# Attention in bursts of seven energy tiles: fewer periods, one movable accumulator bank

## The chip, the cores and the metric

The kernel runs on one core of one Trainium2 chip. Its engines are TensorE (matmuls; its weight loads are counted apart as PEld), VectorE (DVE), ScalarE (ACT), GpSimd (POOL) and SyncE (SP), which here only issues transfers. The metric is the device time of one execution in microseconds (us), from the first to the last instruction. Matrix products land in PSUM, an accumulation memory of eight banks; one bank holds 128 x 512 float32 values. The profile is one execution recorded by the hardware.

## The reference

The input x has 4 images of 64 channels and 96 x 96 pixels, N = 9216 pixels. Two layers follow each other, each preceded by a group normalization. The first is attention over all pairs of pixels, with a sigmoid in place of a softmax, and a channel gate after it:

```python
q = einsum('bchw,oc->bohw', x, wq) + bq   # 8 channels; k likewise, v has 64
energy = einsum('bcn,bcm->bnm', Q, K)     # N x N for each image
att = sigmoid(energy)
out = einsum('bcm,bnm->bcn', V, att) + x
scale = sigmoid(mlp(mean(out)) + mlp(max(out)))
x = x + out * scale
```

The second multiplies 32 x 16 low modes of the image's Fourier transform by complex 64 x 64 weights and transforms back; its result is again added to x. All is float32. The attention is by far the larger part: 4 x 9216 x 9216 sigmoids.

## The kernel before

**Tiling.** Two images make a pair, so there are two pairs (`NPAIR`), with 64 channels of each image on the 128 partitions. A pair's queries are cut into 18 blocks of 512 (`NBLK`, `NB`), which gives 36 blocks in all; its keys into 72 chunks of 128. A block therefore needs 2 x 72 = 144 energy tiles of 128 keys x 512 queries, alternately for one image and the other.

**A period.** The 144 tiles are taken six at a time (`BURST`), 24 bursts to a block and 864 in all. `energies` (L418) issues six matmuls (L424). Each contracts only 32 rows: tile t uses rows 32 * (t % 4) onward, four copies of queries and keys being kept on the four 32-row strips. The six results go to two tiles of three PSUM banks, and two sigmoids on ScalarE (L428), of three banks each, carry them to a buffer `at` in ordinary memory, of which there are two. `attend` (L431) multiplies the values with six sigmoid tiles and adds into an accumulator bank (L435); the tiles of the two images go to its lower and upper 64 partitions. The main loop (L557) issues in period t the energies of burst t + 1, and then the attends of burst t. So the sigmoids of burst t + 1 run beside the attends of burst t.

**The end of a block.** After its last burst VectorE adds the accumulator to x (L578) and takes the maximum (L580).

**Other work.** PSUM has eight banks: six hold energies; the two of the pool `ps_a`, given out by `bank_a` (L357), hold the accumulator and whatever else TensorE has to do. That is written by hand into the lists `mid` (ahead of a period's attends) and `end` (behind them), by period number: keys and values of the chunks (L380, L391), the queries of the next block (L400, three periods ahead of it), normalization and statistics, and, in the second half, the first pair's channel gate and its whole second layer: results (L246), transposes (L258), transform along the width (L267) and the height (L286), mixing with the spectral weights (L186), and the way back (L312, L330). `place` (L508) gives offsets and spacings. The weights of the mixing are loaded into four buffers of 512 KB, four loads a group, ten periods apart (L533); a group's mixing stands six and nine periods behind its load (L535).

The framework places semaphores between engines. It may also reorder instructions that its own model takes to be not ready. What follows the main loop, the second pair's second layer, is a tail of its own.

Of the kernel before, what the change touches and what calls it, by code (L numbers as in the profile page):

```python
# [33 lines left out]
F32 = mybir.dt.float32  # L34
F32R = mybir.dt.float32r
AF = mybir.ActivationFunctionType
ALU = mybir.AluOpType
AX = mybir.AxisListType
PSUM = bass.MemoryType.PSUM

P = 128
B, C, H, W = 4, 64, 96, 96
N = H * W
NPAIR = B // 2
# [3 lines left out]
KH = 32  # L48
NB = 512
NBLK = N // NB  # L50
NCH = N // P
BURST = 6
PART = 3
BURSTS = 2 * NCH // BURST
SIDE = 4
U = KH * KW * 4
UPAD = 4 * SIDE
STRIP = 8 * W
SQ = 32
NSQ = H // SQ  # L60
NSTRIP = N // STRIP
# [16 lines left out]
def tile_kernel(ctx: ExitStack, tc: tile.TileContext, x, cst, late, spec, out):  # L78
    nc = tc.nc
# [10 lines left out]
    xs = []  # L90
# [9 lines left out]
    vT = xpool.tile([P, NCH, P], F32, tag="vT", name="vT")  # L100
# [131 lines left out]
    class Hidden(Layer1):  # L232
# [25 lines left out]
        def transposes(self, r):  # L258

            pt = self.bank(f"pt_{self.p}_{r}")  # L260
            for i in range(4):
                nc.tensor.transpose(pt[:W, bass.ts(i, P)], xs[self.p][:, bass.ts(4 * r + i, W)],  # L262
                                    ident)
            self.xts[r] = self.work.tile([W, NB], F32, tag="xT", bufs=5, name=f"xT_{self.p}_{r}")
            self.move(self.xts[r], pt[:W, :])

        def along_w(self, m):  # L267
# [78 lines left out]
    with tc.tile_pool(name="work", bufs=1) as work, \  # L346
            tc.tile_pool(name="kv", bufs=1) as kvp, \
            tc.tile_pool(name="q", bufs=2) as qp, \
            tc.tile_pool(name="att", bufs=2) as attp, \
            tc.tile_pool(name="ps_s", bufs=1, space=PSUM) as ps_s, \  # L350
            tc.tile_pool(name="ps_a", bufs=2, space=PSUM) as ps_a:

        eb = [ps_s.tile([P, PART, NB], F32, tag=f"e{i}", name=f"e{i}") for i in range(2)]

        kT = kvp.tile([P, NCH // 2, P], F32R, tag="kT", name="kT")

        def bank_a(name):  # L357
            return ps_a.tile([P, NB], F32, tag="a", name=name)

        def halves(src, bias, name):  # L360

# [7 lines left out]
        mark = [None]  # L369
# [6 lines left out]
        def later(step):  # L376
            with tc.issue_after(mark[0].ins):
                step()
# [12 lines left out]
        def values_of(p, s):  # L391
            pp = bank_a(f"pv_{p}_{s}")
            for i in range(4):
                nc.tensor.matmul(pp[:, bass.ts(i, P)], xs[p][:, bass.ts(4 * s + i, P)],  # L394
                                 named("wv"), start=True, stop=True)
            nc.vector.tensor_tensor(  # L396
                vT[:, 4 * s:4 * s + 4, :], pp.rearrange("p (i m) -> p i m", m=P),
                named("bv").unsqueeze(1).to_broadcast([P, 4, P]), ALU.add)
# [16 lines left out]
                    nc.vector.tensor_copy(q[to:to + 32, cols], q[of:of + 32, cols])  # L415
            return q

        def energies(p, n, g, q):  # L418


            for i in range(BURST):
                t = BURST * g + i
                r = 32 * (t % 4)
                nc.tensor.matmul(eb[i // PART][:, i % PART, :], kT[r:r + 32, t // 4, :],  # L424
                                 q[r:r + 32, :], start=True, stop=True)
            at = attp.tile([P, BURST, NB], F32, tag="att", name=f"at_{p}_{n}_{g}")
            for h in range(BURST // PART):
                nc.scalar.activation(at[:, bass.ts(h, PART), :], eb[h], AF.Sigmoid)  # L428
            return at

        def attend(acc, g, at):  # L431
            for i in range(BURST):
                j, b = (BURST * g + i) // 2, i % 2
                half = slice(b * C, (b + 1) * C)
                nc.tensor.matmul(acc[half, :], vT[:, j, half], at[:, i, :],  # L435
                                 start=(j == 0), stop=(j == NCH - 1))

        def stats_of(p):
# [47 lines left out]
        keys(0, 1)  # L486
        values_of(0, 1)

        T = NPAIR * NBLK * BURSTS
        mid = [[] for _ in range(T)]  # L490
        end = [[] for _ in range(T)]
        for s in range(2, NBLK):
            end[s - 2] += [lambda s=s: keys(0, s)]
            mid[s - 1] += [lambda s=s: values_of(0, s)]
            if s + 1 < NBLK:
                end[s - 2] += [lambda s=s: later(norm0[s + 1])]
        each, norm1, mv1 = stats_of(1)
        for i, step in enumerate(each + norm1):
            end[(2 + i // 3) * BURSTS + 2] += [lambda step=step: later(step)]
        last = (NBLK - 1) * BURSTS  # L500
        for s in range(NBLK):
            t = last + -(-(4 * s + 1) // 3)
            end[t] += [lambda s=s: keys(1, s)]
            mid[t + 1] += [lambda s=s: values_of(1, s)]

        first = NBLK * BURSTS

        def place(offset, every, steps):  # L508
            for i, step in enumerate(steps):
                end[first + offset + every * i] += [lambda step=step: later(step)]  # L510

        gate, steps, _ = after(0)
        place(2, 2, steps)
        l1 = Hidden(0, gate, bank_a, lambda dst, src: nc.vector.tensor_copy(dst, src), work)  # L514
        x1d = dram.tile([P, N], F32, tag="x1", name="x1d")
        place(9, 3, [lambda s=s: (l1.result(s), nc.sync.dma_start(
            x1d[:, bass.ts(s, STRIP)], xs[0][:, bass.ts(s, STRIP)])) for s in range(NSTRIP)])
        place(13, 2, [lambda r=r: l1.transposes(r) for r in range(H // 4)])
        place(22, 8, [lambda m=m: l1.along_w(m) for m in range(H // 16)])
        place(64, 2, l1.stats_steps())  # L520

        def workspace():
            ws = xpool.tile([P, N], F32, tag="x0", name="ws")
            l1.ut = ws[:, :U + UPAD]
            at = 2080
            l1.wts = [ws[:, at + 1024 * i:at + 1024 * (i + 1)] for i in range(4)] * (KH // 4)
            l1.vms = [ws[:, at + 4096:at + 5120]] * (KH // 4)
            l1.z = ws[:, at:at + 3072].rearrange("q (h m) -> q h m", m=P)

        place(76, 1, [workspace])  # L530
        place(80, 4, [lambda i=i: l1.along_h(i) for i in range(4)])
        place(98, 1, [l1.constant_mode])
        place(100, 10, [lambda q=q: l1.weights(range(4 * q, 4 * q + 4)) for q in range(KH // 4)])  # L533
        for half in range(2):
            place(106 + 3 * half, 10, [lambda q=q, half=half: l1.mix(q, half)  # L535
                                       for q in range(KH // 4)])
        place(200, 3, [lambda i=i: l1.back_h(i // 4, i // 2 % 2, i % 2) for i in range(8)])
        place(244, 3, [lambda i=i: l1.back_w(i, x1d) for i in range(H // 4)])


        early = []
# [4 lines left out]
            for i, w in enumerate(early):  # L546
                nc.gpsimd.dma_start(w, spec[NSLOT + i])

        place(340, 1, [fetch])
        again = vT.rearrange("p j m -> p (j m)")  # L550
        for s in range(NSTRIP):
            end[T - BURSTS + 2 * s + 1] += [lambda s=s: nc.sync.dma_start(
                again[:, bass.ts(s, STRIP)], xf[bass.ts(1, P), bass.ts(s, STRIP)])]

        at = energies(0, 0, 0, q)
        qn = None
        for t in range(T):  # L557
            p, n, g = t // (NBLK * BURSTS), t // BURSTS % NBLK, t % BURSTS
            nxt = None
            if t + 1 < T:  # L560
                p1, n1, g1 = (t + 1) // (NBLK * BURSTS), (t + 1) // BURSTS % NBLK, (t + 1) % BURSTS
                if g1 == 0:
                    q = qn
                nxt = energies(p1, n1, g1, q)
            for step in mid[t]:
                step()
            if g == 0:
                acc = bank_a(f"acc_{p}_{n}")
            attend(acc, g, at)
            at = nxt  # L570
            if g == BURSTS - 4 and t + 4 < T:
                m = t // BURSTS + 1
                qn = queries(m // NBLK, m % NBLK)
            for step in end[t]:
                step()
            if g == BURSTS - 1:
                blk = xs[p][:, bass.ts(n, NB)]
                nc.vector.scalar_tensor_tensor(blk, acc, 1.0, blk, ALU.mult, ALU.add,  # L578
                                               accum_out=sums[p][:, n:n + 1])
                mark[0] = nc.vector.tensor_reduce(maxs[p][:, n:n + 1], blk, AX.X, ALU.max)  # L580
        gate, steps, f = after(1)
        for step in steps:
            step()
# [2 lines left out]
    with tc.tile_pool(name="tail", bufs=1, reuse_waits="tile") as tail, \  # L586
# [49 lines left out]
        for s in range(NSTRIP):  # L636
# [9 lines left out]
                pa = pa_bank.tile([P, 2 * NB], F32, tag="a", name=f"pa_{n}", bufs=2)  # L646
            v = xt.rearrange("q (h n c) -> q n h c", n=NSQ, c=SQ)
            for k in range(NSQ):
                last = nc.tensor.matmul(pa[:, bass.ts(i, STRIP // NSQ)], fw[:, bass.ts(k, P)], v[:, k],  # L649
                                 start=(k == 0), stop=(k == NSQ - 1))  # L650
            if i < NSTRIP // NSQ - 1:
                continue

# [73 lines left out]
        z = tail.tile([P, P, SQ], F32, tag="z", name="z_1")  # L727
        for i in range(4):
            for b in range(2):
                nc.vector.transpose(z[:H, b * C + i * NO:b * C + (i + 1) * NO, :], pz[b][i][:H, :].rearrange(  # L730
                    "q (k o) -> q o k", o=NO))
        banks.close()
        py_bank = psum("ps_y", 2)
        occupy(2, last, py_bank)
# [100 lines left out]
```

## Time and profile before

The median of three runs is 3196.61 us (3195.66 to 3197.0).

| engine | busy us | share of the span |
|---|---|---|
| TensorE matmuls | 3153.5 | 99% |
| TensorE weight loads, beside matmuls | 1070.9 | 34% |
| ScalarE | 2432.9 | 76% |
| VectorE | 396.4 | 12% |
| GpSimd | 24.5 | 1% |

| group of instructions | number | busy us | mean ns |
|---|---|---|---|
| attends, L435 | 10368 | 2418.1 | 601 |
| sigmoids, L428 | 1728 | 2412.6 | 1448 |
| energies, L424 | 5184 | 636.0 | 461 |
| evacuation of an accumulator, L578 | 36 | 24.9 | 692 |

Each attend is two matmul instructions in the trace (10368 for 5184 tiles). Matmuls overlap, so their mean durations do not add up to time; the distance from one start to the next is what counts. In a timeline line the first number is the start and the second the duration, both in us; the brackets give the idle time of that engine before it, and what ended it.

### The profile page before, as it was taken

The numbers are of one execution on the slowest core, as the hardware profiler recorded it, in microseconds if no ns is written. First come the engines' busy times: TensorE is split into PE (matmuls) and PEld (weight loads), VectorE is DVE, ScalarE is ACT, GpSimd is POOL, SyncE is SP. The second block draws the span as 40 slices with busy tenths as digits, with TensorE's granted clock in tenths as the row PEclk, the third lists the DMA queues.
The fourth block names the chain that finished last, engine by engine and source line by source line (L and its number), as shares of the span: only waits on it lengthen the run. The fifth ranks groups of instructions, "written<-read, shape, count | busy, mean of one in ns | idle before, by whom it ended". The sixth has DMA issues, their size and how long they took to land.

```text
span 3196.5 us, 39125 instructions
## 1 busy us (share of the span) xinstructions
PE 3153.5 (99%) x17490; PEld 1070.9 (34%) x17490; DVE 396.4 (12%) x838; ACT 2432.9 (76%) x1765; POOL 24.5 (1%) x49
## 2 busy tenths in 40 slices
PE   6999999999999999999999999999999999999998
PEld 3333333333333333334333333333333333333336
DVE  4200000000000000002331100000000111000015
ACT  3688888888888888886677777777777777888871
POOL 0000000000000000000000000000000000000001
PEclk9999999999999999999999999999999999999998
DMA  3000000000000000000120100121020102100026
GB/s 139 1 1 1 1 1 1 1 1 1 1 1 1 1 1 1 1 1 1 37 92 17 40 1 30 63 89 37 13 28 10 40 30 70 66 1 1 6 62 221
DMA packets 39145, 88.63 MB, mean 28 GB/s; under 512 B 10336, under 2 KB 17248, under 8 KB 38880
## 3 DMA queue, kind: packets, MB, share of 16 engines
q1 hardware_dynamic: 31856, 61.88, 6.4%
q0 software_dynamic: 5344, 19.27, 1.7%
q10 hardware_dynamic: 1776, 4.97, 0.4%
q8 instruction: 137, 2.24, 0.3%
q14 instruction: 32, 0.26, 0.0%
HBM read 62.77 MB, written 23.33 MB: 27 GB/s over the span
## 4 chain that ended last, share of the span: by engine, by line
PE 98%; DVE 1%; DMA 1%; issue 0%; ACT 0%; POOL 0%; SPq 0%; ACTq 0%
PE acc L435 74%; PE e L424 18%; PE pv L394 1%; PE pv L199 1%; PE py L339 1%; PE pq L405 1%; PE pk L385 1%; DMA x<-in_x_dram 0%; PE py L742 0%; PE pt L262 0%; DVE x L158 0%; DVE xt L641 0%; PE pz L318 0%; PE pu L299 0%; PE pa L272 0%
## 5 line engine op out<-in xcount | busy, mean ns | idle before, releaser
L428 ACT ACTIVATE at<-e 128x1536 f32<-128x1536 f32 x1728 | 2412.6, 1448 | 682.8 <-PE e L424 682.7
L435 PE MATMUL acc<-at,vT 128*64 128x512 f32 x10368 | 2418.1, 601 | 0.0
L435 PEld LDWEIGHTS acc<-at,vT 128*64 128x64 f32 x10368 | 667.8, 136 | 1294.7 <-issue 1279.3
L424 PE MATMUL e<-q,kT 32*128 32x512 f32 x5184 | 636.0, 461 | 1.8 <-ACT at L428 1.3
L424 PEld LDWEIGHTS e<-q,kT 32*128 32x128 f32 x5184 | 257.5, 182 | 642.8 <-issue 595.3
L365 DVE TENSOR_SCALAR full_q<-pq,cs 128x256 f32<-128x256 f32 x36 | 17.4, 484 | 1557.1 <-PE pq L405 1557.0
L578 DVE SCALAR_TENSOR_TENSOR x<-acc,x 128x512 f32<-128x512 f32 x36 | 24.9, 692 | 294.1 <-PE acc L435 294.1
L394 PE MATMUL pv<-cs,x 128*128 128x128 f32 x288 | 42.9, 292 | 0.1
L415 DVE CAST q<-q 32x256 fp32r<-32x256 f32 x144 | 41.0, 285 | 3.8
L341 DVE TENSOR_TENSOR x<-py,x 128x384 f32<-128x384 f32 x24 | 13.4, 558 | 226.0 <-PE py L339 226.0
L394 PEld LDWEIGHTS pv<-cs,x 128*128 128x128 f32 x288 | 35.7, 195 | 14.3 <-DVE full_k L365 12.9
L514 DVE COPY ws<-pv 128x512 f32<-128x512 f32 x16 | 11.1, 691 | 216.4 <-PE pv L199 216.3
L373 DVE SCALAR_TENSOR_TENSOR q<-high_q,cs,full_q 64x256 fp32r<-64x256 f32 x72 | 34.6, 480 | 2.4
L514 DVE COPY xT<-pt 96x512 f32<-96x512 f32 x24 | 16.4, 685 | 114.7 <-PE pt L262 114.7
L365 DVE TENSOR_SCALAR full_k<-pk,cs 128x256 f32<-128x256 f32 x36 | 17.4, 484 | 103.0 <-PE pk L385 103.0
L396 DVE TENSOR_TENSOR vT<-pv,cs 128x512 f32<-128x512 f32 x36 | 24.9, 691 | 8.8 <-PE pv L394 8.8
L580 DVE TENSOR_REDUCE maxs<-x 128x1 f32<-128x512 f32 x36 | 24.7, 685 | 1.1
L385 PE MATMUL pk<-x,cs 128*64 128x256 f32 x144 | 23.3, 395 | 1.5 <-DVE x L145 1.5
L442 DVE BATCH_NORM_STATS2 stats<-x 128x6 f32<-128x512 f32 x36 | 22.3, 679 | 8.1 <-DMA x<-in_x_dram 8.1
L649 PE MATMUL pa<-xt,lc 128*128 128x256 f32 x72 | 19.1, 425 | 3.7 <-DVE xt L641 2.6
L405 PE MATMUL pq<-x,cs 128*64 128x256 f32 x144 | 22.1, 386 | 0.0
L128 PE MATMUL pm_l<-mv_l,cs 128*128 128x1 f32 x8 | 1.7, 286 | 20.6 <-DVE mv_l L124 19.9
(104 smaller groups left out, 457.9 us busy)
## 6 DMA issues: line engine op xcount, KB each, us to landing
ws<-in_spec_dram SPq DMA_DIRECT2D x32, 512.0 KB
x<-in_x_dram SPq DMA_DIRECT2D x15, 512.0 KB
out_dram<-x SPq DMA_DIRECT2D x18, 384.0 KB
w<-in_spec_dram POOLq DMA_DIRECT2D x10, 512.0 KB, 6.6
old<-in_x_dram SPq DMA_DIRECT2D x12, 384.0 KB
x1d<-x SPq DMA_DIRECT2D x12, 384.0 KB
x<-x1d SPq DMA_DIRECT2D x12, 384.0 KB
w_early<-in_spec_dram POOLq DMA_DIRECT2D x9, 512.0 KB, 9.9
```

Of the source, the lines that this page charges most:

```text
L199: self.last = nc.tensor.matmul(pv[bass.ts(g, 32), :].rearrange("q (n k o) -> q n k o", n=SIDE, o=C)[:, :, k, :], self.ut[:, at:at + 32], s ...
L339: nc.tensor.matmul(py[:, :4 * W], self.z[:, i, :], named("gw"), start=True, stop=True)
L365: nc.vector.tensor_scalar(u, src, bias, None, ALU.add)
L373: mark[0] = nc.vector.scalar_tensor_tensor(dst, h.bitcast(F32), is_low, u, ALU.mult, ALU.add)
L385: nc.tensor.matmul(pp[cols, :NB // 2], named("wk")[:, cols], src[:, e, :, :], start=True, stop=True)
L394: nc.tensor.matmul(pp[:, bass.ts(i, P)], xs[p][:, bass.ts(4 * s + i, P)], named("wv"), start=True, stop=True)
L405: nc.tensor.matmul(pq[rows, :half], named("wq")[:, rows], xs[p][:, n * NB + e * half:n * NB + (e + 1) * half], start=True, stop=True)
L415: nc.vector.tensor_copy(q[to:to + 32, cols], q[of:of + 32, cols])
L424: nc.tensor.matmul(eb[i // PART][:, i % PART, :], kT[r:r + 32, t // 4, :], q[r:r + 32, :], start=True, stop=True)
L428: nc.scalar.activation(at[:, bass.ts(h, PART), :], eb[h], AF.Sigmoid)
L435: nc.tensor.matmul(acc[half, :], vT[:, j, half], at[:, i, :], start=(j == 0), stop=(j == NCH - 1))
L514: l1 = Hidden(0, gate, bank_a, lambda dst, src: nc.vector.tensor_copy(dst, src), work)
```

## The change

Bursts get six or seven tiles, by a list for each block: DENSE is 24 sixes, SPARSE 3 sixes and 18 sevens, HALF 10 sixes and 12 sevens. The purpose is to need fewer periods: seven energies take up the four strips twice, just as six do. A burst of seven needs seven energy banks, so all eight banks become one tile: seven for energies, one for the accumulator, and none is left for other work. A burst of six leaves one bank spare, and other work is put only where the next burst has six tiles. Accumulator and spare bank lie at the two ends and change places from block to block; a burst of seven takes the seven banks beside the accumulator. As attends go in pairs, a burst that ends on an odd tile leaves it to the next burst's first pair; `at` becomes one buffer of 14 slots. The sigmoids are split into all but three tiles, and the last three. In the program's order they now follow the first pair of attends, which reads the slot of a carried tile. The other work is placed anew: as `put` finds free periods, in most blocks few, in DENSE and HALF blocks many. The mixing's weights are loaded right behind the mixing of the group before. One of five buffers for transposed rows goes.

```diff
+DENSE = [6] * 24
+HALF = [6 if i % 11 in (0, 2, 4, 6, 8) else 7 for i in range(22)]
+SPARSE = [6 if i in (0, 8, 15) else 7 for i in range(21)]
...
+        banks = ps_s.tile([P, 8, NB], F32, tag="banks", name="banks")
+        spare = [0]
+        at = attp.tile([P, 14, NB], F32, tag="at", name="at")
...
         def bank_a(name):
-            return ps_a.tile([P, NB], F32, tag="a", name=name)
+            return banks[:, spare[0], :]
...
+        def bank_of(t):
+            return 0 if sizes[t] == 7 and block[t] % 2 == 0 else 1
+        def sigmoids(t):
+            of, bank, size = 7 * (t % 2), bank_of(t), sizes[t]
+            for lo, hi in ((0, size - 3), (size - 3, size)):
+                nc.scalar.activation(at[:, of + lo:of + hi, :], banks[:, bank + lo:bank + hi, :],
+                                     AF.Sigmoid)
+        def attend(t, acc, pairs):
+            begin = starts[t] - starts[t] % 2
+            stop = starts[t] + sizes[t]
+            for i in list(range(begin, stop - stop % 2))[pairs]:
...
+        pattern = [DENSE] + [SPARSE] * 16 + [DENSE, DENSE, DENSE, HALF, HALF, HALF, DENSE]
+        pattern += [SPARSE] * (NPAIR * NBLK - len(pattern))
...
+        free = [t for t in range(begins[1], T - 1) if sizes[t + 1] == 6]
+        def put(t, steps, every=1):
+            for step in steps:
+                t = next(f for f in free if f >= t)
+                free.remove(t)
+                mid[t] += [lambda step=step: later(step)]
+                t += every
+            return t
...
-        place(13, 2, [lambda r=r: l1.transposes(r) for r in range(H // 4)])
+        put(first + 9, [lambda r=r: l1.transposes(r) for r in range(H // 4)])
...
-        place(100, 10, [lambda q=q: l1.weights(range(4 * q, 4 * q + 4)) for q in range(KH // 4)])
+        def mixing(q, half):
+            l1.mix(q, half)
+            if half and q + 1 < KH // 4:
+                l1.weights(range(4 * q + 4, 4 * q + 8))
+        t = put(t + 1, [lambda q=q, half=half: mixing(q, half)
+                        for q in range(KH // 4) for half in range(2)])
...
+            acc, spare[0] = banks[:, 7 - n % 2 * 7, :], n % 2 * 7
             if t + 1 < T:
+                energies(t + 1, q)
             for step in mid[t]:
                 step()
+            attend(t, acc, slice(0, 2))
+            if t + 1 < T:
+                sigmoids(t + 1)
+            attend(t, acc, slice(2, None))
             for step in end[t]:
                 step()
```

More of the change, by code (lines that the diff above doesn't have):

```diff
@@ L51 @@
 NCH = N // P
-BURST = 6
-PART = 3
-BURSTS = 2 * NCH // BURST
+TILES = 2 * NCH
+DENSE = [6] * 24
+HALF = [6 if i % 11 in (0, 2, 4, 6, 8) else 7 for i in range(22)]
+SPARSE = [6 if i in (0, 8, 15) else 7 for i in range(21)]
 SIDE = 4
@@ L263, in transposes @@
                                     ident)
-            self.xts[r] = self.work.tile([W, NB], F32, tag="xT", bufs=5, name=f"xT_{self.p}_{r}")
+            self.xts[r] = self.work.tile([W, NB], F32, tag="xT", bufs=4, name=f"xT_{self.p}_{r}")
             self.move(self.xts[r], pt[:W, :])
@@ L348, in tile_kernel @@
             tc.tile_pool(name="q", bufs=2) as qp, \
[L349 to L353, printed above, removed]
+            tc.tile_pool(name="att", bufs=1) as attp, \
+            tc.tile_pool(name="ps_s", bufs=1, space=PSUM) as ps_s:
+        banks = ps_s.tile([P, 8, NB], F32, tag="banks", name="banks")
+        spare = [0]
+        at = attp.tile([P, 14, NB], F32, tag="at", name="at")
         kT = kvp.tile([P, NCH // 2, P], F32R, tag="kT", name="kT")
         def bank_a(name):
-            return ps_a.tile([P, NB], F32, tag="a", name=name)
+            return banks[:, spare[0], :]
         def halves(src, bias, name):
@@ L416, in queries, with energies @@
             return q
[L418 to L424, printed above, removed]
-                                 q[r:r + 32, :], start=True, stop=True)
[L426 to L433, printed above, removed]
+        def bank_of(t):
+            return 0 if sizes[t] == 7 and block[t] % 2 == 0 else 1
+        def energies(t, q):
+            for i in range(starts[t], starts[t] + sizes[t]):
+                r = 32 * (i % 4)
+                nc.tensor.matmul(banks[:, bank_of(t) + i - starts[t], :], kT[r:r + 32, i // 4, :],
+                                 q[r:r + 32, :], start=True, stop=True)
+        def sigmoids(t):
[7 more added lines that the diff above has]
+            for i in list(range(begin, stop - stop % 2))[pairs]:
+                j, b = i // 2, i % 2
                 half = slice(b * C, (b + 1) * C)
-                nc.tensor.matmul(acc[half, :], vT[:, j, half], at[:, i, :],
+                of = (7 * (t % 2) + i - starts[t] if i >= starts[t] else
+                      7 * ((t - 1) % 2) + sizes[t - 1] - 1)
+                nc.tensor.matmul(acc[half, :], vT[:, j, half], at[:, of, :],
                                  start=(j == 0), stop=(j == NCH - 1))
@@ L487, in tile_kernel @@
         values_of(0, 1)
-        T = NPAIR * NBLK * BURSTS
+        pattern = [DENSE] + [SPARSE] * 16 + [DENSE, DENSE, DENSE, HALF, HALF, HALF, DENSE]
+        pattern += [SPARSE] * (NPAIR * NBLK - len(pattern))
+        sizes = [size for sz in pattern for size in sz]
+        starts = [sum(sz[:i]) for sz in pattern for i in range(len(sz))]
+        block = [n for n, sz in enumerate(pattern) for _ in sz]
+        T = len(sizes)
+        begins = [block.index(n) for n in range(NPAIR * NBLK)] + [T]
         mid = [[] for _ in range(T)]
         end = [[] for _ in range(T)]
+        free = [t for t in range(begins[1], T - 1) if sizes[t + 1] == 6]
[6 more added lines that the diff above has]
+            return t
+        ask = {}
+        for n in range(1, NPAIR * NBLK):
+            t = begins[n] - 4
+            if pattern[n - 1] is DENSE:
+                end[t] += [lambda n=n: ask.update({n: queries(n // NBLK, n % NBLK)})]
+            else:
+                t = [f for f in free if f < begins[n] - 1][-1]
+                free.remove(t)
+                mid[t] += [lambda n=n: ask.update({n: queries(n // NBLK, n % NBLK)})]
         for s in range(2, NBLK):
@@ L497, in tile_kernel @@
         each, norm1, mv1 = stats_of(1)
-        for i, step in enumerate(each + norm1):
-            end[(2 + i // 3) * BURSTS + 2] += [lambda step=step: later(step)]
-        last = (NBLK - 1) * BURSTS
+        for i, step in enumerate(each):
+            if i <= NBLK:
+                end[begins[1 + i // 4] + 2 + i % 4] += [lambda step=step: later(step)]
+            else:
+                put(begins[6 + i - NBLK], [step])
+        for i, step in enumerate(norm1):
+            end[begins[10 + i // 4] + 2 + i % 4] += [lambda step=step: later(step)]
         for s in range(NBLK):
-            t = last + -(-(4 * s + 1) // 3)
+            t = begins[NBLK - 1] - -(4 * s + 1) // 3
             end[t] += [lambda s=s: keys(1, s)]
             mid[t + 1] += [lambda s=s: values_of(1, s)]
[L506 to L510, printed above, removed]
+            if t + 1 in free:
+                free.remove(t + 1)
+        first = begins[NBLK]
         gate, steps, _ = after(0)
-        place(2, 2, steps)
+        end[first + 1] += [lambda: later(steps[0])]
+        put(first + 2, steps[1:], 2)
         l1 = Hidden(0, gate, bank_a, lambda dst, src: nc.vector.tensor_copy(dst, src), work)
         x1d = dram.tile([P, N], F32, tag="x1", name="x1d")
-        place(9, 3, [lambda s=s: (l1.result(s), nc.sync.dma_start(
-            x1d[:, bass.ts(s, STRIP)], xs[0][:, bass.ts(s, STRIP)])) for s in range(NSTRIP)])
-        place(13, 2, [lambda r=r: l1.transposes(r) for r in range(H // 4)])
-        place(22, 8, [lambda m=m: l1.along_w(m) for m in range(H // 16)])
-        place(64, 2, l1.stats_steps())
+        for s in range(NSTRIP):
+            end[first + 7 + 2 * s] += [lambda s=s: later(lambda: (
+                l1.result(s), nc.sync.dma_start(x1d[:, bass.ts(s, STRIP)],
+                                                xs[0][:, bass.ts(s, STRIP)])))]
+        put(first + 9, [lambda r=r: l1.transposes(r) for r in range(H // 4)])
+        for m in range(H // 16):
+            end[first + 12 + 4 * m] += [lambda m=m: later(lambda: l1.along_w(m))]
+        t = put(first + 36, l1.stats_steps(), 2)
         def workspace():
@@ L528, in workspace @@
             l1.z = ws[:, at:at + 3072].rearrange("q (h m) -> q h m", m=P)
-        place(76, 1, [workspace])
-        place(80, 4, [lambda i=i: l1.along_h(i) for i in range(4)])
-        place(98, 1, [l1.constant_mode])
-        place(100, 10, [lambda q=q: l1.weights(range(4 * q, 4 * q + 4)) for q in range(KH // 4)])
[L534 to L538, printed above, removed]
+            l1.weights(range(4))
+        end[t] += [workspace]
+        t = put(t + 2, [lambda i=i: l1.along_h(i) for i in range(4)], 2)
+        end[t] += [lambda: later(l1.constant_mode)]
+        def mixing(q, half):
[4 more added lines that the diff above has]
+                        for q in range(KH // 4) for half in range(2)])
+        t = put(t + 5, [lambda i=i: l1.back_h(i // 4, i // 2 % 2, i % 2) for i in range(8)])
+        t = put(t + 5, [lambda i=i: l1.back_w(i, x1d) for i in range(H // 4)])
         early = []
@@ L547, in fetch @@
                 nc.gpsimd.dma_start(w, spec[NSLOT + i])
-        place(340, 1, [fetch])
+        assert t + 30 < T
+        end[t + 30] += [fetch]
         again = vT.rearrange("p j m -> p (j m)")
         for s in range(NSTRIP):
-            end[T - BURSTS + 2 * s + 1] += [lambda s=s: nc.sync.dma_start(
+            t = next(t for t in range(begins[-2], T)
+                     if starts[t] + sizes[t] >= 2 * (STRIP // P) * (s + 1))
+            end[t] += [lambda s=s: nc.sync.dma_start(
                 again[:, bass.ts(s, STRIP)], xf[bass.ts(1, P), bass.ts(s, STRIP)])]
-        at = energies(0, 0, 0, q)
@@ L556, in tile_kernel @@
-        qn = None
+        energies(0, q)
+        sigmoids(0)
         for t in range(T):
-            p, n, g = t // (NBLK * BURSTS), t // BURSTS % NBLK, t % BURSTS
-            nxt = None
+            n = block[t]
+            acc, spare[0] = banks[:, 7 - n % 2 * 7, :], n % 2 * 7
             if t + 1 < T:
[L561 to L564, printed above, removed]
+                if starts[t + 1] == 0:
+                    q = ask[n + 1]
+                energies(t + 1, q)
@@ L565, in tile_kernel @@
             for step in mid[t]:
                 step()
[L567 to L573, printed above, removed]
+            attend(t, acc, slice(0, 2))
+            if t + 1 < T:
+                sigmoids(t + 1)
+            attend(t, acc, slice(2, None))
             for step in end[t]:
                 step()
-            if g == BURSTS - 1:
-                blk = xs[p][:, bass.ts(n, NB)]
+            if t + 1 == begins[n + 1]:
+                p, m = divmod(n, NBLK)
+                blk = xs[p][:, bass.ts(m, NB)]
@@ L578, in tile_kernel @@
                 nc.vector.scalar_tensor_tensor(blk, acc, 1.0, blk, ALU.mult, ALU.add,
-                                               accum_out=sums[p][:, n:n + 1])
-                mark[0] = nc.vector.tensor_reduce(maxs[p][:, n:n + 1], blk, AX.X, ALU.max)
+                                               accum_out=sums[p][:, m:m + 1])
+                mark[0] = nc.vector.tensor_reduce(maxs[p][:, m:m + 1], blk, AX.X, ALU.max)
         gate, steps, f = after(1)
@@ L648, in tile_kernel @@
             for k in range(NSQ):
-                last = nc.tensor.matmul(pa[:, bass.ts(i, STRIP // NSQ)], fw[:, bass.ts(k, P)], v[:, k],
-                                 start=(k == 0), stop=(k == NSQ - 1))
+                last = nc.tensor.matmul(pa[:, bass.ts(i, STRIP // NSQ)], fw[:, bass.ts(k, P)],
+                                        v[:, k], start=(k == 0), stop=(k == NSQ - 1))
             if i < NSTRIP // NSQ - 1:
@@ L729, in tile_kernel @@
             for b in range(2):
-                nc.vector.transpose(z[:H, b * C + i * NO:b * C + (i + 1) * NO, :], pz[b][i][:H, :].rearrange(
-                    "q (k o) -> q o k", o=NO))
+                nc.vector.transpose(z[:H, b * C + i * NO:b * C + (i + 1) * NO, :],
+                                    pz[b][i][:H, :].rearrange("q (k o) -> q o k", o=NO))
         banks.close()
```

## The prediction

> **What bounds the kernel now.** I read the page first (engine totals, chain, costly groups), then the timeline of a few periods, then two places where an engine is late.
>
> ```profile
> PE 3153.5 (99%) x17490; PEld 1070.9 (34%) x17490; DVE 396.4 (12%) x838; ACT 2432.9 (76%) x1765; POOL 24.5 (1%) x49
> ...
> PE acc L435 74%; PE e L424 18%; PE pv L394 1%; PE pv L199 1%; PE py L339 1%; PE pq L405 1%; PE pk L385 1%; DMA x<-in_x_dram 0%; PE py L742 0%; PE pt L262 0%; DVE x L158 0%; DVE xt L641 0%; PE pz L318 0%; PE pu L299 0%; PE pa L272 0%
> ...
> L428 ACT ACTIVATE at<-e 128x1536 f32<-128x1536 f32 x1728 | 2412.6, 1448 | 682.8 <-PE e L424 682.7
> ```
>
> TensorE is the bound: the chain is its energies (L424) and attends (L435), 92% together. ScalarE has 682.8 us of idle time, but all of it waits for energies: 0.6 us in each of 864 periods. It is therefore second in line, and the timeline says by how little:
>
> ```profile
> 143.23 0.30 PEld L424 LDWEIGHTS e<-q,kT 32*128 32x128 f32 x6 [0.81 <-issue]
> ...
> 143.35 0.69 DVE L578 SCALAR_TENSOR_TENSOR x<-acc,x 128x512 f32<-128x512 f32 x1 [7.07 <-PE acc L435]
> 143.84 2.79 ACT L428 ACTIVATE at<-e 128x1536 f32<-128x1536 f32 x2 [0.59 <-PE e L424]
> ...
> 143.90 2.79 PE L435 MATMUL acc<-at,vT 128*64 128x512 f32 x12
> 143.97 0.08 DVE L578 DVE_READ_ACCUMULATOR x<-acc,x 128x1 f32 x1
> ...
> 146.62 0.30 PEld L424 LDWEIGHTS e<-q,kT 32*128 32x128 f32 x6 [0.81 <-issue]
> ```
>
> A period is 146.62 - 143.23 = 3.39 us: energies until the attends start at 143.90 (0.66), then attends. Both sigmoids of the burst end at 143.84 + 2.79 = 146.63, within 0.01 us of the next burst's start. A late sigmoid is seen once here:
>
> ```profile
> 1288.73 0.19 PEld L424 LDWEIGHTS e<-q,kT 32*128 32x128 f32 x3 [0.81 <-issue]
> ...
> 1289.07 0.19 PEld L424 LDWEIGHTS e<-q,kT 32*128 32x128 f32 x3 [0.16 <-ACT at L428]
> ...
> 1289.50 0.20 PEld L435 LDWEIGHTS acc<-at,vT 128*64 128x64 f32 x4 [0.24 <-PE e L424]
> ```
>
> The preceding sigmoid ended 0.29 after 1288.73 (1287.58 + 1.45 in the same view). The waiting weight load came 0.05 later and the attends 0.43 after that load, at +0.77 instead of +0.66. So 0.05 and 0.43 are the prices of a late bank.
>
> **What the Trainium skill says.** "TensorE: Matmul & The Clock Gate", "The mechanism" of Part 3: small matmuls on different 32-row strips run together, and weights load beside running matmuls only where the strip differs. The trace agrees: four energies start within 0.07 us at 500.72, the other two at 501.06, and the attends at 501.38. Six energies are two rounds (4+2), and so are seven (4+3). The same page's "What overlaps and what doesn't" says matmuls keep their order, so one that waits holds all behind it, as at 1289.07. "ScalarE: Activation LUTs", "What ACT_TABLE_LOAD costs": 0.833 ns per element, neighbours overlapping by some 93 ns. Here a 1536-element sigmoid takes 1.45 and the pair 2.79, so the second starts 1.35 after the first: 0.10 of overlap, in agreement. "PSUM — Partial Sum Buffer", "Terms": TensorE must not write a bank while another engine reads it. So each reuse of a bank is a real wait.
>
> **The change, part by part.** *Fewer periods.* The lists in the diff give 5x24 + 28x21 + 3x22 = 774 bursts (the short description says 776); I use 774, 90 fewer. Attends go in pairs, and one pair costs 0.857 (two steps of 0.43 between weight loads; three are 2.57). The rest of a period, 3.387 - 2.571 = 0.816, is fixed: the two rounds and the two switches. Every tile is still attended and seven energies cost no third round. Saved: 90 x 0.816 = 73.4 us.
>
> *Sigmoids of seven tiles.* They are now 4 + 3 tiles. The first takes 512 x 0.833 = 0.43 more, so it lasts 1.87 and the second starts 1.35 + 0.43 = 1.77 after it. ScalarE starts 0.61 after the energies (143.23 to 143.84) and ends at 0.61 + 1.77 + 1.45 = 3.83. A seven-burst that starts on an even tile attends six tiles (the odd one is carried), one that starts on an odd tile attends eight. So TensorE returns for the next burst after 3.39 and 4.24 by turns. After 4.24 ScalarE is done. After 3.39 it lacks 0.44: the first round is free, because the first sigmoid has ended, but the banks of the second round are not. Their weights load at 0.44 + 0.05 = 0.49, the attends start at 0.49 + 0.43 = 0.92 instead of 0.66: **0.26 lost in each short period behind a seven-burst**. Queued behind that wait are the attends, and all of TensorE with them; the next long period cannot give it back, as TensorE had no idle time there. Walking the lists, I count 281 such periods (9 in nearly every block of 21). 281 x 0.263 = 73.9. From both sides: 0.155, if a late second round needs only the 0.32 that an undisturbed one takes from 501.06 to 501.38; 0.35, if the scheduler puts an attend pair into the gap (two switches more). In block 0 it does move matmuls so: energies are split 4+2 around the values. I take the measured price, 0.263. The interval for the sum is 44 to 98.
>
> A check by the cycle: 14 tiles as two sevens take 3.387 + 0.263 + 4.244 = 7.89; as sixes 14/6 x 3.387 = 7.90. The gain and the wait are one size.
>
> *The accumulator changes places.* The first burst of a block has six tiles, the second has seven in 31 blocks. That second burst needs the bank of the block just ended, and its energies are issued directly behind that block's last attends. VectorE empties this bank from 143.35 to 144.04, with the accumulator read until 144.05: at +0.82, plus 0.05 for the release, 0.87 after TensorE wants it. In 16 even blocks the first energy is the one that waits: 0.87. In 15 odd ones it is the seventh: 0.87 + 0.43 - 0.66 = 0.64. Sum 13.9 + 9.6 = 23.5. From both sides: 0 if attends of the new block are pulled ahead of it, about 0.95 each (29) if the release waits still longer. I take 23.5.
>
> *Mixing work moved closer.* Other work using the spare bank now sits only where the next burst has six tiles. Its number of matmuls is unchanged. Normalizing, queries and statistics find 3 to 20 us beside attends: nothing. The exception is the weights of the spectral mixing:
>
> ```profile
> 2038.72 1.07 PE L199 MATMUL pv<-ws 128*32 128x256 f32 x16
> ```
> ```profile
> 2046.00:2048.00 2.00, 2.00 (x14) 0.64 (x12) 0.00 (x0) 1.41 (x2) 0.00 (x0) 1.00 0.97 369
> 2048.00:2050.00 2.00, 2.00 (x14) 0.55 (x12) 0.00 (x0) 1.90 (x2) 0.00 (x0) 1.00 0.21 86
> 2050.00:2052.00 2.00, 2.00 (x14) 0.78 (x16) 0.00 (x0) 1.50 (x2) 0.00 (x0) 1.00 0.00 0
> ```
>
> The last column of the second view is GB/s: from the last mixing of a group to the landing of the next 2 MB there are about 10.0 us (2038.7 to 2048.7), hidden before because groups lay ten periods apart. In the changed lists six of the seven gaps are two periods, 2 x 3.39 + half a pair + the mixing's own 1.07 + some 0.13 of waits = 8.4. TensorE would stand 1.7 us in five, and some 4.3 in the one where the store-and-reload transfers of the intermediate are queued ahead: 13 us. Bounds: 0 if the scheduler puts attends first, 25 if transfers queue badly. Transposes and the first transform of the second layer now lie in neighbouring periods on one spare bank: six waits of about 0.3, 2 us. One tile buffer less for transposes, the 14-slot attend buffer (its carried slot is read by the first pair, at 1.8, before the second sigmoid at 2.4), prologue and tail: nothing.
>
> Sum: 3196.6 - 73.4 + 73.9 + 23.5 + 13 + 2 = **3235.6**, say 3235.
>
> **Rivals.** (a) *The late sigmoid is not felt*, as when the energies of the second round had slack: the purpose is met, 3196.6 - 73.4 + 23.5 + 13 + 2 = 3162, or 3123 without any of the new waits. For it: ScalarE has 0.6 us of idle in each period. Against: that idle is the latency from energies to sigmoid, which each period pays again. (b) *The wait is partly hidden*: 0.155 each and no wait on weights: 3196.6 - 73.4 + 43.6 + 23.5 + 2 = 3192, or 3205 with those waits; near no change. For it: only the late weight load of a single strip was seen. Against: the second round uses strips whose loads wait in just that way. (c) *The scheduler fills the gaps with attend pairs*: 281 + 31 switches of 0.35, 109, so 3196.6 - 73.4 + 109 + 13 + 2 = 3247. For it: block 0. Against: in the quiet periods of before it never splits the six.
>
> **How the numbers follow.** Forecast (3212 to 3262) 0.52; (c) 0.15; (b) 0.15; (a) 0.18. The range, 3175 to 3275, leaves out (a) and little above, 2 in 10. Faster: (a) and the low end of (b), 0.20. Same within 0.2% (3190 to 3203): about half of (b), 0.08. Slower: 0.72.
>
> **What would show it.** Energies split by a wait on ScalarE after about every second seven-burst, with 0.26 us from it; ScalarE's idle share down and its wait for energies shorter; a wait of energies on L578's evacuation near 0.9 us at block starts; TensorE idle on the weights near the mixing. If short periods take 3.39 and not 3.65, the sigmoid step is wrong; if the block starts show attends ahead of energies, the accumulator step is.

## The result, and the profile after

The changed kernel takes 3251.3 us (median of four runs, 3250.6 to 3251.91), the kernel before beside it 3196.1: a ratio of 1.0173 (95% interval 1.0155 to 1.019), 55 us slower. The forecast was 3235, with a range of 3175 to 3275.

First the page of the kernel after, the lines that answer to those of before: the engine totals, and the sigmoids with ScalarE's idle time.

```profile
PE 3196.3 (98%) x17490; PEld 1085.7 (33%) x17490; DVE 396.6 (12%) x838; ACT 2413.5 (74%) x1585; POOL 24.5 (1%) x49
...
L436 ACT ACTIVATE at<-banks 128x1536 f32<-128x1536 f32 (+1 forms) x1548 | 2393.3, 1597 | 758.1 <-PE banks L430 744.9
```

TensorE has the same 17490 matmuls and is the bound as before, yet counts 43 us more as busy. ScalarE has 180 sigmoid instructions fewer and a lower share. A reader of totals alone would not suspect ScalarE. The timeline of the kernel after, over one short and one long period of a quiet block, tells more (start, duration, engine, line):

```profile
505.67 0.30 PEld L430 LDWEIGHTS banks<-q,kT 32*128 32x128 f32 x7 [0.81 <-issue]
505.67 0.73 PE L430 MATMUL banks<-q,kT 32*128 32x512 f32 x7
506.27 3.22 ACT L436 ACTIVATE at<-banks 128x2048 f32<-128x2048 f32 x2 [0.59 <-PE banks L430]
506.33 0.20 PEld L449 LDWEIGHTS banks<-at,vT 128*64 128x64 f32 x4 [0.36 <-issue]
...
509.06 0.19 PEld L430 LDWEIGHTS banks<-q,kT 32*128 32x128 f32 x4 [0.81 <-issue]
...
509.54 0.19 PEld L430 LDWEIGHTS banks<-q,kT 32*128 32x128 f32 x3 [0.29 <-ACT at L436]
509.68 3.22 ACT L436 ACTIVATE at<-banks 128x2048 f32<-128x2048 f32 x2 [0.19 <-PE banks L430]
509.97 0.20 PEld L449 LDWEIGHTS banks<-at,vT 128*64 128x64 f32 x4 [0.25 <-issue]
...
513.56 0.30 PEld L430 LDWEIGHTS banks<-q,kT 32*128 32x128 f32 x7 [0.81 <-ACT at L436]
...
514.17 3.22 ACT L436 ACTIVATE at<-banks 128x2048 f32<-128x2048 f32 x2 [1.28 <-PE banks L430]
```

At 505.67 seven energies go in one run and the attends follow at 506.33, 0.66 later: no third round. Their sigmoids run from 506.27 to 509.49. TensorE is back at 509.06, after 3.39 us. Its first four energies go, and the last three wait until 509.54, 0.05 behind the sigmoid. The attends start at 509.97, at +0.91 instead of +0.66. The long period that follows ends at 513.56, 4.50 after 509.06: 4.24 plus those 0.25, which are not given back. (Counted from attends to attends, as the prediction's 3.65 is, the short period takes 509.97 - 506.33 = 3.64.)

Two block starts of the kernel after, the first of an odd block, the second of an even one:

```profile
144.84 0.30 PEld L430 LDWEIGHTS banks<-q,kT 32*128 32x128 f32 x6 [0.81 <-issue]
...
144.95 0.69 DVE L629 SCALAR_TENSOR_TENSOR x<-banks,x 128x512 f32<-128x512 f32 x1 [7.08 <-PE banks L449]
...
145.70 0.18 PEld L430 LDWEIGHTS banks<-q,kT 32*128 32x128 f32 x1 [0.57 <-DVE x L629]
146.13 0.20 PEld L449 LDWEIGHTS banks<-at,vT 128*64 128x64 f32 x4 [0.24 <-issue]
```
```profile
227.16 0.19 PEld L430 LDWEIGHTS banks<-q,kT 32*128 32x128 f32 x4 [0.81 <-issue]
...
228.03 0.19 PEld L430 LDWEIGHTS banks<-q,kT 32*128 32x128 f32 x3 [0.68 <-DVE x L629]
...
228.47 0.20 PEld L449 LDWEIGHTS banks<-at,vT 128*64 128x64 f32 x4 [0.25 <-issue]
...
228.63 1.88 ACT L436 ACTIVATE at<-banks 128x2048 f32<-128x2048 f32 x1 [2.58 <-PE banks L430]
```

In both, energies wait for VectorE's evacuation until 0.86 or 0.87 after TensorE wanted the bank. In the odd block it is the one energy of that bank. In the even block four energies go first all the same and three wait. The attends start at +1.29 and +1.31, about 0.64 late. In the even block the first sigmoid starts only at 228.63, since it needs the late bank; in the trace the second round of the next burst is then some 0.47 late instead of 0.25.

The whole trace of after can be summed in this way. In 763 of the 774 bursts the energies go in one run; in 314 of these the next kind of work on TensorE, mostly attends, starts over 0.1 us later than 0.66 after the first energy, 97.8 us in all. In the trace of before there are 5 such bursts, 0.6 us in all. By size, 263 of the 314 lie between 0.2 and 0.28, 16 near 0.47, and 31 (the block starts) between 0.6 and 0.7.

A block without other work (a quiet block) tells the same in the distance between first attends of neighbouring blocks. It was 81.72 us and is now 82.34 in odd and 82.52 in even blocks in most such blocks. Most of the 55 us lies in blocks 18 to 31, which hold the first pair's second layer: together they take 1260.4 us instead of 1218.8. There the mixing (L201) looks like this, TensorE alone:

```profile
1815.33 1.07 PE L201 MATMUL banks<-ws 128*32 128x256 f32 x16
1816.33 2.79 PE L449 MATMUL banks<-at,vT 128*64 128x512 f32 x12
...
1823.32 0.62 PE L201 MATMUL banks<-ws 128*32 128x256 f32 x2
1823.87 2.79 PE L449 MATMUL banks<-at,vT 128*64 128x512 f32 x10
1826.59 0.62 PE L201 MATMUL banks<-ws 128*32 128x256 f32 x2
...
1829.43 0.62 PE L201 MATMUL banks<-ws 128*32 128x256 f32 x2
1829.98 0.50 PE L430 MATMUL banks<-q,kT 32*128 32x512 f32 x3
...
1831.42 1.05 PE L201 MATMUL banks<-ws 128*32 128x256 f32 x10
```

The next mixing is due 8.0 us after 1815.33. TensorE does not stand still for it: the mixing comes in pieces of 2, 2, 2 and 10 matmul instructions, with attends and energies between. A piece of two takes 0.55 until the next kind of work starts (1823.32 to 1823.87); sixteen in one take 1.00 (1815.33 to 1816.33). In the code the first four matmuls of a mixing, of two instructions each, read the four weight buffers one after another, and the later ones read them again. That fits the pieces: one for each of the first three transfers, and the rest behind the fourth. The pieces do not follow the landing itself: the last one starts at 1831.42, while the transfers, at 328 GB/s from 1821 to 1825, are down to 39 GB/s from 1825 to 1827 and to 0 from 1829.

### The profile page after: what moved, and what is told of

It is laid out like the page before. It is cut to its first block, busy times and chain, and to the rows that moved or that the text cites. A ratio compares the mean times of both kernels' runs of the same rounds, so it can differ in the third digit from the quotient of the medians.

```text
span 3250.1 us, 39517 instructions
## 1 busy us (share of the span) xinstructions
PE 3196.3 (98%) x17490; PEld 1085.7 (33%) x17490; DVE 396.6 (12%) x838; ACT 2413.5 (74%) x1585; POOL 24.5 (1%) x49
## 4 chain that ended last, share of the span: by engine, by line
PE 94%; DVE 2%; issue 1%; DMA 1%; ACT 1%; SPq 0%; POOL 0%; ACTq 0%; DVEq 0%
PE banks L449 71%; PE banks L430 18%; PE banks L399 1%; ACT at L436 1%; PE banks L201 1%; DVE x L629 1%; PE banks L410 1%; PE banks L341 1%; PE banks L390 1%; DMA x<-in_x_dram 0%; PE py L793 0%; DVE x L160 0%; PE pv L201 0%; PE banks L264 0%; DMA old<-in_x_dram 0%
## 5 line engine op out<-in xcount | busy, mean ns | idle before, releaser
L436 ACT ACTIVATE at<-banks 128x1536 f32<-128x1536 f32 (+1 forms) x1548 | 2393.3, 1597 | 758.1 <-PE banks L430 744.9
L449 PE MATMUL banks<-at,vT 128*64 128x512 f32 x10368 | 2416.0, 600 | 0.0
L449 PEld LDWEIGHTS banks<-at,vT 128*64 128x64 f32 x10368 | 680.6, 136 | 1277.0 <-issue 1268.3
L430 PE MATMUL banks<-q,kT 32*128 32x512 f32 x5184 | 659.2, 471 | 11.1 <-DVE x L629 5.8
L430 PEld LDWEIGHTS banks<-q,kT 32*128 32x128 f32 x5184 | 260.5, 182 | 727.1 <-ACT at L436 353.5
L370 DVE TENSOR_SCALAR full_q<-banks,cs 128x256 f32<-128x256 f32 x36 | 17.4, 483 | 1346.2 <-PE banks L410 1346.2
L629 DVE SCALAR_TENSOR_TENSOR x<-banks,x 128x512 f32<-128x512 f32 x36 | 24.9, 691 | 649.0 <-PE banks L449 649.0
L399 PE MATMUL banks<-cs,x 128*128 128x128 f32 x288 | 43.8, 297 | 1.3 <-DVE full_q L370 0.6
L399 PEld LDWEIGHTS banks<-cs,x 128*128 128x128 f32 x288 | 36.5, 199 | 15.6 <-DVE full_k L370 13.6
L557 DVE COPY ws<-banks 128x512 f32<-128x512 f32 x16 | 11.1, 691 | 164.1 <-PE banks L201 141.2
L370 DVE TENSOR_SCALAR full_k<-banks,cs 128x256 f32<-128x256 f32 x36 | 17.4, 484 | 103.8 <-PE banks L390 103.8
L201 PE MATMUL banks<-ws 128*32 128x256 f32 x256 | 28.2, 387 | 0.0
L390 PE MATMUL banks<-x,cs 128*64 128x256 f32 x144 | 23.3, 395 | 1.5 <-DVE x L147 1.5
L410 PE MATMUL banks<-x,cs 128*64 128x256 f32 x144 | 23.7, 408 | 0.6 <-DVE full_k L370 0.6
L557 DVE COPY xT<-banks 96x512 f32<-96x512 f32 x24 | 16.4, 682 | 47.7 <-PE banks L264 47.7
```

Source lines behind the costliest of these rows:

```text
L201: self.last = nc.tensor.matmul(pv[bass.ts(g, 32), :].rearrange("q (n k o) -> q n k o", n=SIDE, o=C)[:, :, k, :], self.ut[:, at:at + 32], s ...
L370: nc.vector.tensor_scalar(u, src, bias, None, ALU.add)
L390: nc.tensor.matmul(pp[cols, :NB // 2], named("wk")[:, cols], src[:, e, :, :], start=True, stop=True)
L410: nc.tensor.matmul(pq[rows, :half], named("wq")[:, rows], xs[p][:, n * NB + e * half:n * NB + (e + 1) * half], start=True, stop=True)
L430: nc.tensor.matmul(banks[:, bank_of(t) + i - starts[t], :], kT[r:r + 32, i // 4, :], q[r:r + 32, :], start=True, stop=True)
L436: nc.scalar.activation(at[:, of + lo:of + hi, :], banks[:, bank + lo:bank + hi, :], AF.Sigmoid)
```

## Experiments

The theory: the 90 periods saved are worth their 73 us, and three new waits take back more than that, the largest being the late second sigmoid. Rivals to it: one of the other two is the whole cause, or the saving itself is smaller. All runs were made beside the kernel before; it was at 3195.9 to 3196.3.

**Run 1, sevens with a shorter second sigmoid.** The edit, at L436 (the buffer is zeroed once at the start):

```diff
+                n = NB // 2 if lo else NB
-                nc.scalar.activation(at[:, of + lo:of + hi, :], banks[:, bank + lo:bank + hi, :],
+                nc.scalar.activation(at[:, of + lo:of + hi, :n], banks[:, bank + lo:bank + hi, :n],
                                      AF.Sigmoid)
```

> The kernel after, with the second sigmoid of each burst taking only the first 256 of its 512 columns (the other columns of those tiles stay zero, so part of the attention is left out). ScalarE then ends 768 x 0.833 = 0.64 us sooner, 0.2 us before the shortest period is over. Theory (the late second sigmoid costs 0.25 us in each of 281 short periods): 281 x 0.25 = 70 us less than after, 3181 us, below the kernel before. Rival (the loss comes from the accumulator's place and the other work, and the sigmoids end in time): no change, 3251 us.

Measured: 3176.3 us, ratio to before 0.9938 (0.9921 to 0.9954), and 75.0 less than after. In its timeline, a short period between two sevens:

```profile
502.78 0.30 PEld L431 LDWEIGHTS banks<-q,kT 32*128 32x128 f32 x7 [0.81 <-issue]
...
503.39 2.58 ACT L438 ACTIVATE at<-banks 128x2048 f32<-128x2048 f32 x2 [1.67 <-PE banks L431]
...
506.17 0.30 PEld L431 LDWEIGHTS banks<-q,kT 32*128 32x128 f32 x7 [0.81 <-ACT at L438]
...
506.83 3.65 PE L451 MATMUL banks<-at,vT 128*64 128x512 f32 x16
```

The sigmoids end at 505.97, TensorE returns at 506.17 and all seven energies go at once; the attends start 0.66 later. Of the late starts, 39 with 22.6 us are left, 75.2 us fewer. So the wait is worth what the sum of its occurrences says: it alone takes as much as the 73 us forecast for the saving. The block starts (31 of the 39) and the other work still cost what they did.

**Run 2, the control: the same in the kernel before** (there each burst's second sigmoid of three tiles takes 256 columns, by the same edit).

> The kernel before with the same shortened second sigmoid (the same part of the attention left out): a control. Theory: with bursts of six ScalarE is in time, so nothing changes: 3196 us within 2 us. Rival (ScalarE already holds the energies up before the change, as the fourth energy waits 0.06 us for it in nearly every period): 864 x 0.06 = 50 us less, 3146 us.

Measured: 3197.4, ratio 1.0003 (0.9995 to 1.0012): no change. With sixes ScalarE is in time, and the fourth energy's 0.06 us costs nothing. A warning comes with it, the table of waits of TensorE's weight loads in this control (us in total, times, longest):

```profile
PEld e L427 <- ACT at L432: 570.9, 700, 3.1
```

570.9 us stand against ScalarE here, in the kernel before only 46.0, and the time is the same. The idle time of the weight loader is charged to what released it last, though most of it passes beside running matmuls. The kernel after shows 353.5 us in that row, and its loss is 75.

**Run 3, two sixes at the start of a block.**

```diff
-SPARSE = [6 if i in (0, 8, 15) else 7 for i in range(21)]
+SPARSE = [6 if i in (0, 1, 15) else 7 for i in range(21)]
```

> The kernel after with the sixes of a SPARSE block at places 0, 1 and 15 instead of 0, 8 and 15, so that the second burst of the block no longer needs the bank of the block before. Theory (energies wait for the evacuation of the old accumulator, 0.87 us in even and 0.64 us in odd blocks, 28 blocks): about 21 us less, 3230 us. Rival (the scheduler hides the evacuation behind attends): no change, 3251 us.

Measured: 3233.9, ratio 1.0116 (1.0101 to 1.0131), 17.4 less than after. The evacuation is felt, 0.62 us a block over 28 blocks; the scheduler does not hide it. In both traces most quiet blocks have nine late second rounds, so moving the six changes little else there.

**Run 4, all bursts of six, new places.**

```diff
-        pattern = [DENSE] + [SPARSE] * 16 + [DENSE, DENSE, DENSE, HALF, HALF, HALF, DENSE]
-        pattern += [SPARSE] * (NPAIR * NBLK - len(pattern))
+        pattern = [DENSE] * (NPAIR * NBLK)
...
-                        for q in range(KH // 4) for half in range(2)])
+                        for q in range(KH // 4) for half in range(2)], 2)
```

> The kernel after with DENSE blocks only: no sevens, 864 periods, but the single tile of eight banks, the movable accumulator and the new placing by free periods, with the mixing every second period as in the HALF blocks of after. Theory A (other work moved closer costs some 25 us, because the mixing is cut into pieces around the landing of its weights): 3222 us. Theory B (it costs the 13 to 15 us of the prediction): 3210 us. Rival (the placing costs nothing, and all 55 us come from the sevens): 3197 us.

Measured: 3230.2, ratio 1.0107 (1.0092 to 1.0123), 34 us more than before and 8 more than the higher theory. In its trace most blocks without other work, in both halves, take the same time as before to 0.01 us, so the one tile of banks and the accumulator's change of place cost nothing by themselves. The excess is nearly all in the blocks of the second layer. Seven times, once for each group after the first, a mixing is cut up:

```profile
1889.83 0.62 PE L201 MATMUL banks<-ws 128*32 128x256 f32 x2
1890.38 2.79 PE L449 MATMUL banks<-at,vT 128*64 128x512 f32 x12
1893.10 0.50 PE L430 MATMUL banks<-q,kT 32*128 32x512 f32 x1
1893.53 0.62 PE L201 MATMUL banks<-ws 128*32 128x256 f32 x2
...
1900.14 0.73 PE L430 MATMUL banks<-q,kT 32*128 32x512 f32 x6
```

The two periods from 1889.17 (six energies, just ahead of these lines) to 1900.14 take 10.97 us; two plain periods and a mixing in one piece take 2 x 3.387 + 1.00 = 7.77. That is 3.2 us, and seven times that is 22. The way back (L320, L341) is cut up too: in this trace its periods take some 8 us more than the sum of their parts, most of the rest.

**Run 5, as run 4, the weights loaded once.**

```diff
         def mixing(q, half):
             l1.mix(q, half)
-            if half and q + 1 < KH // 4:
-                l1.weights(range(4 * q + 4, 4 * q + 8))
```

> The kernel with all bursts of six and the new placing (run before: 3230 us), but the mixing's weights are loaded once and used for all eight groups, so that seven of eight groups are mixed with wrong weights; all else as it was. Theory (the mixing is cut into pieces, each with switches on TensorE, because it is placed two periods behind the load of its weights): about 20 us less, 3210 us. Rival (the pieces come from the crowding of other work on one spare bank, whatever the weights): no change, 3230 us.

Measured: 3208.4, ratio 1.0039 (1.0024 to 1.0054), 21.8 less than run 4. In its trace the mixings stand in pieces of sixteen again. So the cuts of the mixing, and 22 of the 34 us, come from the weights under way and not from crowding on the spare bank. The remaining 12 us do not come from the weights.

**Run 6, as run 4, the work spaced.**

```diff
-        t = put(t + 1, [lambda q=q, half=half: mixing(q, half)
-                        for q in range(KH // 4) for half in range(2)])
-        t = put(t + 5, [lambda i=i: l1.back_h(i // 4, i // 2 % 2, i % 2) for i in range(8)])
-        t = put(t + 5, [lambda i=i: l1.back_w(i, x1d) for i in range(H // 4)])
+        for r in range(KH // 4):
+            t = put(t + 1, [lambda r=r: mixing(r, 0)], 3)
+            t = put(t, [lambda r=r: mixing(r, 1)], 6)
+        t = put(t + 5, [lambda i=i: l1.back_h(i // 4, i // 2 % 2, i % 2) for i in range(8)], 3)
+        t = put(t + 5, [lambda i=i: l1.back_w(i, x1d) for i in range(H // 4)], 3)
```

> All bursts of six, with the new bank layout, but the mixing spaced as in the kernel before (three and seven periods) and the way back in every third period. Theory (the 34 us of the closer placing are all crowding; the one tile of banks and the movable accumulator cost nothing): 3198 us, as before. Rival (the single spare bank, or the work ahead of the attends, costs by itself): 3210 us or more.

Measured: 3199.7, ratio 1.0011 (1.0004 to 1.0018). Of the 34 us, 31 are gone with the spacing. The transposes were not spaced; in this trace their periods lose 3.1 us to waits for the spare bank (shown further down for the kernel after). That is the size of the 3 left, but no run takes these waits away.

**Run 7, runs 1 and 3 together.**

> Sevens, with both the shortened second sigmoid (part of the attention left out) and the sixes at places 0, 1 and 15. Theory (the two waits add up): 3176 - 17 = 3159 us. Rival (they overlap at the block starts): some 3166 us or more.

Measured: 3160.4, ratio 0.989 (0.9873 to 0.9906), 15.8 less than run 1. The two waits add up, to within 1.6 us of run 3's 17.4.

**Run 8, run 7 with the weights loaded once.**

> As the previous one, and the mixing's weights loaded only once (wrong weights for seven of eight groups): sevens with all three suspected waits taken away. Theory (90 periods fewer save 73 us, and the three waits are what takes it back): 3159 - 20 = 3139 us, some 16 above the 3123 that the saving alone gives, for what is left of the crowding. Rival (the sevens save less than 0.816 us a period): 3155 us or more.

Measured: 3133.1, ratio 0.9803 (0.9788 to 0.9817), 27.4 less than run 7. With all three taken away it lies 10 us above 3196.3 - 73.4 = 3122.9. The quiet blocks show the saving without the crowding. Such a block takes 81.72 us in before, 82.34 or 82.52 in after, 80.0 in run 1, 81.7 in run 3, and 79.33 in runs 7 and 8. That is 2.39 less than before for three periods fewer, 0.80 for each, where 0.816 was forecast; for 90 periods it makes 72 us.

**Run 9, nothing left out: sevens only where it is quiet.**

```diff
-        pattern = [DENSE] + [SPARSE] * 16 + [DENSE, DENSE, DENSE, HALF, HALF, HALF, DENSE]
-        pattern += [SPARSE] * (NPAIR * NBLK - len(pattern))
+        pattern = [DENSE] + [SPARSE] * 16 + [DENSE] * 15 + [SPARSE] * 4
```

with the sixes of run 3 and the spacing of run 6.

> Nothing left out: sevens only in the 20 blocks without other work (with the sixes at 0, 1 and 15), sixes in the others, and the other work spaced as in the run with 3200 us. Theory (in quiet blocks the 3 periods saved, 2.45 us, and the 9 late sigmoids, 9 x 0.25 = 2.3 us, cancel): 3200 us within 4 us, no gain over the kernel before. Rival (with the other two waits out of the way the sevens pay, as they were meant to): 20 x 2.45 = 49 us less, 3151 us, which would beat both kernels.

Measured: 3199.3, ratio 1.0009 (1.0003 to 1.0016), the time of run 6. Twenty blocks of sevens, without the block-start wait and away from other work, gain nothing and lose nothing. None of these versions that leaves nothing out beats the kernel before.

## Why the prediction was right, step by step

| step | forecast, us | measured, us | from |
|---|---|---|---|
| 90 periods fewer | -73.4 | -72 | quiet blocks of runs 7 and 8 |
| late second sigmoid | +73.9 | +75.0 | run 1 against after |
| accumulator at block starts | +23.5 | +15.8 in 28 of 31 blocks, +1.9 in the other three | run 7 against run 1; trace of run 8 |
| mixing near its weights | +13 | +27.4 | run 8 against run 7 |
| transposes | +2 | about +3 | traces of after and before, no run |
| way back in pieces | none | about +4 | trace of run 8, no run |

The measured column adds up to the 55 us found. The forecast was 16 us too low, mostly by the mixing.

*The saving* held: seven energies take two rounds, attends start at +0.66, and a period fewer is worth 0.80.

*The late second sigmoid* held in mechanism, price and number: forecast 0.26 us in 281 periods; by the trace 75.2 us in the 275 late starts that run 1 takes away. The sum over fourteen tiles came out too: two sevens cost what fourteen tiles in sixes cost, and run 9 shows it for whole blocks. One reading of the prediction is loose: 682.7 us of ScalarE's waits over 864 periods are 0.79 each, and only in a period without other work are they 0.59. Nothing in the sum rests on it.

*The block starts* held in mechanism. Two sizes differ. The release came as forecast (0.87 wanted, 0.86 and 0.87 seen), but in even blocks the scheduler sends four energies ahead of the waiting one, so the first loss is 0.65 and not 0.87, and the next burst loses 0.47 instead of 0.26. That the two errors nearly cancel, 1.12 against 1.13, is luck. In the trace of after the block starts come to 31 times 0.64 and 16 times 0.2, some 23 us, as forecast. About 3 of these are in run 1's 75.0, since the shorter sigmoid takes the 0.47 away too; the 17.4 of run 3, for 28 blocks, is some 3 less than their share of the 23, and that difference was not traced.

*The mixing* is the term that was mis-sized, and its mechanism was wrong as well. The times behind it were right: the weights landed after about 10 us, and the next mixing was due after 8.0, with 8.4 forecast. But TensorE doesn't stand until they land. The mixing is cut into pieces with other work between, and each cut pays switches from one kind of matmul to another: some 4.6 us a group in after (27.4 / 6) where 2.1 were forecast (13 / 6). I had used this reordering as a reason for the lower bound, zero; it made things dearer.

*The small waits of the transposes* are in the trace, and of the size forecast (six of 0.3, 2 us). Where nothing waits, a transpose adds 0.57 to a period and a transform 1.00, before and after alike. Behind a transform the next transpose must wait until VectorE has emptied the one spare bank (L557):

```profile
1621.38 0.29 PEld L430 LDWEIGHTS banks<-q,kT 32*128 32x128 f32 x6 [0.84 <-issue]
1621.52 0.69 DVE L557 COPY ae<-banks 128x512 f32<-128x512 f32 x1 [3.07 <-PE banks L274]
...
1622.26 0.39 PEld L264 LDWEIGHTS banks<-cs,x 128*96 128x96 f32 x4 [0.59 <-DVE ae L557]
```

The transpose starts 0.88 after the energies instead of 0.66. There are five waits of 0.22 (in one of them VectorE is emptying the old accumulator), one of 0.56, and one period, in which a transform waits for the queries and cuts energies and attends in two, takes 1.43 more: 3.1 in all, against 0.1 in the trace of before. *The way back* stood nowhere in the forecast. Its first steps after follow each other in successive periods and come in pieces; in the trace of run 8 its periods take 4.2 us more than the sum of their parts. Runs 4 to 6 show this cost for sixes; for sevens it was only seen in the trace.

Of the signs named ahead, two were wrong. TensorE is not idle near the mixing, as told above. And ScalarE's wait for energies is longer than before, 744.9 against 682.7 us, not shorter, and its idle share is up. In the long periods it is done early and waits 1.28 us (from 509.68 + 3.22 = 512.90 until the sigmoid at 514.17) instead of 0.59; an idle total cannot show that it is late in every other period.

Rival (a), the late sigmoid not felt, fell with run 1. Rival (b), the wait partly hidden, fell with the 0.25 at 509.97. Rival (c), attends put into the gaps, fell because in 763 of 774 bursts no other work stands between the energies.

## What to carry to other kernels

When two engines take turns on the same buffers, a longer batch saves the bound engine's switches only while the second engine's whole batch still fits into its shortest turn; compare these two times, start to end, and not the engines' busy shares. Where turns alternate in length, as here, the short one decides, and the slack of the long one is worth nothing. Work that needs a fresh transfer belongs further behind its load than the transfer takes, because a scheduler that fills the gap with other work may pay more in switches than the gap is long, as it did here (4.6 us a group, where the gap was forecast at some 2).

## What the runs showed that was not expected

The idle time that the profile charges to ScalarE on the weight loader and the time lost to it have no fixed relation: 46.0 and 570.9 us with no loss, 353.5 us with a loss of 75. And small pieces of a matmul group are dear: three pieces of two, at 0.55 us each, cost 1.65 us of TensorE, more than the group of sixteen in one piece with its 1.00.
